# A four-layer graph network with a planned instruction order: layer 3 gathered by nodes, one flip through HBM, norms on ScalarE, scalings on GpSimd

## The chip, the cores and the metric

The kernel runs on one core of a Trainium2 chip. The core has TensorE (PE, with weight loads listed as PEld), VectorE (DVE), ScalarE (ACT), GpSimd (POOL) and the queues of SyncE (SP), which issue most of the DMAs here. The metric is device time in microseconds of one execution: 2461.91 us before, the median of three (2461.11 to 2462.0). Everything is fp32.

## The reference

There are 16 graphs (batches) of N = 1024 nodes with D = 128 features, and an adjacency with weights, about 1.6% of it nonzero. Four layers follow one another; each takes the layer-normed and ReLU'd state and adds its result to the state x, all per batch:

```
h = relu(layernorm(x))
layer 0, three times:  h = h @ W + b;  nh = h / |h|
                       h = (adj * (nh nh^T)) @ h;  relu but in the last;       x += h
layer 1:               x += mask * (relu(((1 + eps) h + adj^T h) @ W1 + b1) @ W2 + b2)
layer 2:               g = h @ W; attention over adj > 0 of tanh(g a1 + g a2), softmax;  x += attn @ g
layer 3:               g = h @ W^T + b;  e = g A g^T, plus its transpose
                       att = softmax(e where adj > 0 else 0, over the first node axis) * adj
                       hp = relu(att @ g)
                       i, f, o = sigmoid([h, hp] . w + b), three gates for each node
                       x += o * tanh(sigmoid(i * hp + f * h))
```

In layer 3 the three gates need, for each node, the dot product of hp with three rows of 128 weights (the second halves of the gate weights).

## The kernel before

**Tiles.** A batch's state is one tile of 128 partitions by 1024: eight blocks of 128 nodes, nodes on partitions, features along the row. Where a product needs features on partitions the tile is flipped: `flipped` (L619) transposes eight blocks on TensorE (L562) into PSUM and takes them out with two ScalarE evictions (L615). `squares` (L566) does the same by another way: it writes the tile to HBM, reads it back in 32 by 32 squares and turns the squares with one VectorE transpose. The adjacency lies in SBUF as eight row tiles adjT (128 x 1024, turned by the same trick on loading, `turn`, L859), and for layer 1 as loaded (adjL).

**The loops.** For each batch, `layer0` to `layer3` run over eight blocks j. In layers 0 and 3 `Square.row` (L741) makes a row of a symmetric product in two PSUM tiles of 128 x 512 (L753), taking blocks below the diagonal from already computed ones, by transposes on TensorE (L763) from copies `above`, or, in the middle batches, through HBM (`by_hbm`, `got`). VectorE multiplies that row with adjT into a tile ew or e (L952, L1169), and TensorE gathers it. There are two ways to gather. `accumulate` (L810) holds h of block j as weights and streams 512 columns of e twice: the result comes out with features on partitions. `accumulate_nodes` (L820) holds one 128 x 128 block of e at a time as weights and streams 128 columns of h, eight times: the result comes out with nodes on partitions. Layer 3 uses the first, so its result hpT must be turned back: `project` (L587) multiplies it with eye3, an identity with the three gate weight columns beside it (131 columns), which gives hp and the gates' dot products at once (psN, L1213), and ScalarE copies them out (L1216).

**Norms and gates.** `layernorm` (L653) takes statistics on VectorE (L663, L672), the power -1/2 on GpSimd (rstd, L555), and scales the first four blocks on VectorE (L691) and the other four on ScalarE with the ReLU inside (L698); `relu` (L712) does the ReLU of the first four. Layer 0's row norms rn are powers on GpSimd too. Layer 2 adds `alone` times hn to x, for nodes without neighbours (L1035, L637). Layer 3's `finish` (L1225) makes the gates (L1237, L1261, L1262), multiplies hn with f on GpSimd (L1265), then i * hp + z and o * z + x: on VectorE, eight `scalar_tensor_tensor` each (L1255), and in the last two batches on GpSimd (L1248, L1249). Then the result leaves by DMA. In the last batch this goes in two halves. In the last two batches GpSimd also multiplies the odd rows e with adjT (L1190).

**The order of the work.** Nothing is issued as written. Every operation goes into a `Plan` (L54) with an engine and an estimated time, the planner chooses a static order for each engine, and the program is emitted in that order. Ready operations are ranked by a deadline of the batch (PERIOD, LAST), less the length of what follows them, less a lead from the table LEADS. Buffers come from pools (POOLS) with a limit in all, and one for batches younger than the oldest unfinished (KINDS). An operation with `port` set shares a resource with GpSimd's in the plan: it places no two of them at one time. FLAGS are letters that switch variants; before they are "Cabcdkxhyz".

## Time and profile before

| | busy us | share of the span of 2462.7 us |
|---|---|---|
| TensorE matmuls | 2397.5 | 97% |
| VectorE | 2106.1 | 86% |
| ScalarE | 1291.5 | 52% |
| GpSimd | 254.5 | 10% |

A line of the groups reads: the line of the code, the engine, the operation, output <- inputs with their shapes, how many; then the busy time in all and the mean in ns; then the idle time ahead of it and who ended it. A line of the chain or the timeline begins with its start and its length in us. An fp32 matmul stands as two records with a weight load each, so counts of matmuls are twice those of the code; transposes stand as one. Lines of the profile are those of the kernel before.

### The profile page before, as it was taken

The numbers are of one execution on the slowest core, as the hardware profiler recorded it, in microseconds if no ns is written. First come the engines' busy times: TensorE is split into PE (matmuls) and PEld (weight loads), VectorE is DVE, ScalarE is ACT, GpSimd is POOL, SyncE is SP. The second block draws the span as 40 slices with busy tenths as digits, with TensorE's granted clock in tenths as the row PEclk, the third lists the DMA queues.
The fourth block names the chain that finished last, engine by engine and source line by source line (L and its number), as shares of the span: only waits on it lengthen the run. The fifth ranks groups of instructions, "written<-read, shape, count | busy, mean of one in ns | idle before, by whom it ended". The sixth has DMA issues, their size and how long they took to land.

```text
span 2462.7 us, 34845 instructions
## 1 busy us (share of the span) xinstructions
PE 2397.5 (97%) x11946; PEld 1592.9 (65%) x11946; DVE 2106.1 (86%) x5232; ACT 1291.5 (52%) x2404; POOL 254.5 (10%) x155
## 2 busy tenths in 40 slices
PE   6999999999999999999999999999999999999985
PEld 3568576775756657576675766657576675765763
DVE  6758889888998989899898998989899898897585
ACT  4415564735546465464644646465464745656274
POOL 1001010100101101010010101101010010100025
PEclk9999999999999999999999999999999999999998
DMA  8731929658394764928649394774929646072000
GB/s 132 125 103 35 167 56 144 139 89 160 72 159 112 107 142 94 174 67 147 136 82 167 65 164 114 100 145 93 173 73 146 134 86 133 28 96 75 26 1 18
DMA packets 1129473, 263.35 MB, mean 107 GB/s; under 512 B 971856, under 2 KB 1112912, under 8 KB 1129296
## 3 DMA queue, kind: packets, MB, share of 16 engines
q1 hardware_dynamic: 1108368, 251.73, 57.3%
q10 hardware_dynamic: 20928, 9.40, 1.4%
q8 instruction: 94, 1.54, 0.3%
q14 instruction: 83, 0.68, 0.1%
HBM read 198.14 MB, written 62.91 MB: 106 GB/s over the span
## 4 chain that ended last, share of the span: by engine, by line
PE 86%; DVE 5%; DMA 4%; ACT 3%; SPq 1%; POOL 1%; issue 0%; POOLq 0%; DVEq 0%; ACTq 0%
PE acc L815 33%; PE sq L753 17%; PE acc L826 17%; PE psP L593 6%; PE sq L763 4%; PE py L1014 2%; PE py L603 2%; PE ps_hTn L562 2%; DMA adjT<-in_adj_dram 1%; DMA by_hbm<-above 1%; PE ps_hnT L562 1%; PE pg L603 1%; DVE ew L952 1%; PE psN L593 1%; SPq L872 1%; DMA got<-by_hbm 1%
## 5 line engine op out<-in xcount | busy, mean ns | idle before, releaser
L952 DVE SCALAR_TENSOR_TENSOR ew<-sq,rn,adjT 128x512 f32<-128x512 f32 x612 | 437.9, 741 | 92.8 <-ACT above L785 33.0
L815 PE MATMUL acc<-ew,h 128*128 128x512 f32 x1024 | 488.0, 598 | 8.6 <-DVE ew L952 8.3
L753 PE MATMUL sq<-hTn 128*128 128x512 f32 (+3 forms) x1152 | 432.3, 488 | 0.4 <-ACT hTn L615 0.3
L785 ACT COPY above<-sq 128x384 f32<-128x384 f32 (+3 forms) x432 | 167.6, 392 | 431.8 <-PE sq L763 257.4
L753 PEld LDWEIGHTS sq<-hTn 128*128 128x128 f32 x1152 | 198.8, 191 | 152.6 <-issue 104.3
L815 PEld LDWEIGHTS acc<-ew,h 128*128 128x128 f32 x1024 | 177.7, 191 | 164.8 <-issue 120.9
L555 POOL TENSOR_TENSOR rstd<-ve,mhalf 128x8 f32<-128x8 f32 x64 | 107.5, 1679 | 1572.5 <-DVE ve L674 1524.3
L826 PEld LDWEIGHTS acc<-h,ew 128*128 128x128 f32 x2048 | 243.1, 192 | 29.9 <-issue 17.3
L826 PEld LDWEIGHTS acc<-h,e 128*128 128x128 f32 x2048 | 240.5, 194 | 25.6 <-issue 13.3
L826 PE MATMUL acc<-h,ew 128*128 128x128 f32 x2048 | 252.3, 276 | 0.9 <-DVE ew L952 0.9
L826 PE MATMUL acc<-h,e 128*128 128x129 f32 x2048 | 243.1, 277 | 3.4 <-DVE e L1102 3.4
L815 PE MATMUL acc<-e,hs 128*128 128x512 f32 x512 | 242.1, 595 | 0.5 <-DVE e L1194 0.5
L883 ACT ACTIVATE adjT<-adjT 128x1024 f32<-128x1024 f32 x128 | 135.2, 1057 | 203.8 <-DVE adjT L880 136.2
L815 PE MATMUL acc<-adjL,hn 128*128 128x512 f32 x512 | 229.6, 593 | 0.1
L763 PEld LDWEIGHTS sq<-ident,above 128*128 128x128 f32 x960 | 125.2, 141 | 122.1 <-issue 79.2
L1185 ACT ACTIVATE e<-e,top 128x1024 f32<-128x1024 f32 x128 | 146.8, 1147 | 105.3 <-DVE top L1181 103.6
L763 PE MATMUL sq<-ident,above 128*128 128x128 f32 x960 | 175.5, 274 | 5.5 <-ACT above L785 5.4
L1102 DVE SCALAR_TENSOR_TENSOR e<-adjT,e 128x512 f32<-128x512 f32 x256 | 161.5, 685 | 14.6 <-ACT e L1098 14.4
L880 DVE STREAM_TRANSPOSE adjT<-adjT 128x1024 f32<-128x1024 f32 x128 | 154.5, 1223 | 14.5 <-DMA adjT<-in_adj_dram 13.9
L775 DVE STREAM_TRANSPOSE above<-sq 128x512 f32<-128x512 f32 x208 | 147.3, 709 | 21.6 <-PE sq L753 19.6
L815 PEld LDWEIGHTS acc<-adjL,hn 128*128 128x128 f32 x512 | 93.9, 190 | 102.8 <-issue 88.1
L1194 DVE TENSOR_TENSOR e<-e,adjT 128x512 f32<-128x512 f32 x240 | 157.2, 686 | 0.0
(129 smaller groups left out, 3534.2 us busy)
## 6 DMA issues: line engine op xcount, KB each, us to landing
adjT<-in_adj_dram SPq DMA_DIRECT2D x512, 128.0 KB, 4.2
adjL<-in_adj_dram SPq DMA_DIRECT2D x128, 512.0 KB, 5.0
by_hbm<-above SPq DMA_DIRECT2D x104, 512.0 KB, 4.1
got<-by_hbm SPq DMA_DIRECT2D x416, 128.0 KB, 3.9
x<-in_x_dram SPq DMA_DIRECT2D x15, 512.0 KB, 5.4
out_dram<-z ACTq DMA_DIRECT2D x15, 512.0 KB, 5.9
x<-in_x_dram SPq DMA_DIRECT2D x2, 256.0 KB, 4.4
out_dram<-z ACTq DMA_DIRECT2D x2, 256.0 KB, 2.3
```

What stands on the lines that cost most here:

```text
L593: nc.tensor.matmul(dst.t[:, (c - lo) * n : (c - lo + 1) * n], cols(srcT.t, c), w, start=True, stop=True)
L753: lambda: nc.tensor.matmul(dst.t[:, (first - lo) * P :], cols(leftT.t, j), span(rightT.t, first, hi), start=True, stop=True),
L763: nc.tensor.transpose(cols(dst.t, r), cols(above.t, p), ident)
L775: lambda: nc.vector.transpose(span(above.t, p, p + 4), read.t),
L785: lambda: nc.scalar.copy(span(above.t, p, p + hi - first), read.t[:, (first - lo) * P :]),
L815: lambda s=s, lo=lo, hi=hi: nc.tensor.matmul(acc[s].t, cols(h.t, at, w), span(ew.t, lo, hi), start=(j == 0), stop=(j == NB - 1)),
L826: nc.tensor.matmul(a.t[:, (c - lo) * n : (c - lo + 1) * n], cols(ew.t, c), h.t[:, j * w : j * w + n], start=(j == 0 and c == lo), stop=(j ...
L880: dve(V(N), [t], [t], lambda t=t: nc.vector.transpose(t.t, t.t), True)
L952: lambda view=view, ew=ew, rn=rn, j=j, lo=lo, hi=hi: nc.vector.scalar_tensor_tensor(by_block(span(ew.t, lo, hi), D, 4), view(), rn.t[:, j ...
L1102: lambda e=e, j=j, lo=lo, hi=hi: nc.vector.scalar_tensor_tensor(span(e.t, lo, hi), span(aT[j].t, lo, hi), 0.0, span(e.t, lo, hi), op0=ALU. ...
L1185: lambda e=e, top=top, tot=tot: nc.scalar.activation(e.t[:, 0:N], e.t[:, 0:N], AF.Exp, bias=top.t, accum_out=tot.t),
L1194: lambda e=e, j=j, lo=lo, hi=hi: nc.vector.tensor_mul(span(e.t, lo, hi), span(e.t, lo, hi), span(aT[j].t, lo, hi)),
```

## The change

Five letters come in by FLAGS, and "y" goes, as P takes in what it did:

- **E**: in batches 0 to 13 layer 3 is gathered by nodes. hp comes out with nodes on partitions, so the eight products with eye3 and their copies go. The gates' dot products are made by three GpSimd multiplications of hp with a weight row (wh3, loaded once, repeated over the blocks), each with a VectorE sum along the features.
- **R**: norms are scaled on ScalarE alone, eight activations with the ReLU inside; the separate ReLU goes.
- **P**: layer 2's `alone` and layer 3's two scalings run on GpSimd, as a multiplication and an addition over the whole tile, but for the last batch's layer 3.
- **D**: from batch 2 on layer 0's first flip is made through HBM, by `squares`.
- **T**: in the last batch layer 3's scalings and the odd rows' multiplications run on VectorE; batch 14 keeps them on GpSimd.

It is for taking work from TensorE and VectorE and giving it to the engines with idle time. The plan's numbers change with it: the pools, limits, PERIOD, LAST, WINDOW, some estimates of GpSimd times, and the whole table of leads, which is left out here.

```diff
--- before.py
+++ after.py
@@ -288,6 +288,7 @@
 
         return loaded(group, name, [P, n], src.partition_broadcast(P))
 
+    FLAGS = set("CabcdkxhERPDzT")
     R = B * NB
     w0, b0 = [], []
     for i, (w, v) in enumerate(((L0_W0, L0_b0), (L0_W1, L0_b1), (L0_W2, L0_b2))):
@@ -312,12 +313,16 @@
     w3e = const.tile([D, E3], F32, name="w3e")
     b3e = const.tile([P, E3], F32, name="b3e")
     eye3 = const.tile([D, E3], F32, name="eye3")
+
+    wh3 = const.tile([P, 3 * D], F32, name="wh3") if "E" in FLAGS else None
     load_const(third, b3e[:, 0:D], L3_W_b.partition_broadcast(P))
     for g, (w, v) in enumerate(((L3_ig_w, L3_ig_b), (L3_fg_w, L3_fg_b), (L3_og_w, L3_og_b))):
         at = slice(D + g, D + g + 1)
         load_const(third, w3e[:, at], w[0, 0:D].rearrange("(p o) -> p o", o=1))
         load_const(third, eye3[:, at], w[0, D : 2 * D].rearrange("(p o) -> p o", o=1))
         load_const(third, b3e[:, at], v.partition_broadcast(P))
+        if "E" in FLAGS:
+            load_const(third, wh3[:, g * D : (g + 1) * D], w[0, D : 2 * D].partition_broadcast(P))
     for load_it in first:
         load_it()
     maskf = const.tile([R, P], F32, name="maskf")
@@ -330,136 +335,137 @@
     bg = const.tile([D, 1], F32, name="bg")
 
 
-    POOLS = {"adjT": 16, "adjL": 5, "x": 3, "big": 13, "above": 2, "got": 1, "bank": 8, "small": 29, "row": 8, "hbm": 3, "hrow": 2}
+    POOLS = {"adjT": 16, "adjL": 5, "x": 3, "big": 13, "above": 2, "got": 1, "bank": 8, "small": 22, "row": 6, "hbm": 3, "hrow": 2}
     KINDS = {
-        "adjT": ("adjT", 16, 16), "adjL": ("adjL", 5, 5), "x": ("x", 3, 3), "w4": ("big", 10, 6),
-        "chunk": ("big", 12, 4), "above": ("above", 2, 1), "got": ("got", 1, 1), "ps": ("bank", 8, 8),
-        "acc": ("bank", 8, 8), "small": ("small", 7, 6), "row": ("row", 4, 2), "hbm": ("hbm", 3, 2),
+        "adjT": ("adjT", 16, 16), "adjL": ("adjL", 5, 5), "x": ("x", 3, 3), "w4": ("big", 9, 5),
+        "chunk": ("big", 13, 9), "above": ("above", 2, 1), "got": ("got", 1, 1), "ps": ("bank", 7, 7),
+        "acc": ("bank", 6, 6), "small": ("small", 7, 7), "row": ("row", 5, 2), "hbm": ("hbm", 3, 2),
         "hrow": ("hrow", 2, 1),
     }
-    PERIOD, LAST, AHEAD, WINDOW = 60.0, 9.0, 2, 0.05
+    PERIOD, LAST, AHEAD, WINDOW = 108.0, 34.0, 2, 0.02
 
     LEADS = {
...
     }
     plan = Plan(POOLS, KINDS, lambda b: min(b * PERIOD, (B - 2) * PERIOD + LAST), AHEAD, WINDOW, LEADS)
     now = [0, ""]
@@ -514,7 +520,6 @@
 
 
 
-    FLAGS = set("Cabcdkxhyz")
 
     LO, HI = 1, 2
     TINY = 0.09
@@ -648,7 +653,7 @@
 
         v = lambda: by_block(a.t, w)[:, :, 0:D]
         pool_op(1.9, [a, scalar], [a], lambda: nc.gpsimd.tensor_mul(v(), v(), per_node(of_node())))
-        pool_op(1.9, [a, b], [dst], lambda: nc.gpsimd.tensor_add(by_block(dst.t), v(), by_block(b.t)))
+        pool_op(2.37, [a, b], [dst], lambda: nc.gpsimd.tensor_add(by_block(dst.t), v(), by_block(b.t)))
 
     def layernorm(k, xt, behind=None):
 
@@ -817,20 +822,20 @@
                 ),
             )
 
-    def accumulate_nodes(acc, parts, h, j, w, n, ew):
+    def accumulate_nodes(acc, parts, h, at, w, n, ew, j):
 
         for a, (lo, hi) in zip(acc, parts):
 
             def emit(a=a, lo=lo, hi=hi):
                 for c in range(lo, hi):
                     nc.tensor.matmul(
-                        a.t[:, (c - lo) * n : (c - lo + 1) * n], cols(ew.t, c), h.t[:, j * w : j * w + n],
+                        a.t[:, (c - lo) * n : (c - lo + 1) * n], cols(ew.t, c), h.t[:, at * w : at * w + n],
                         start=(j == 0 and c == lo), stop=(j == NB - 1), skip_group_check=True,
                     )
 
             pe(
                 (hi - lo) * (MM_BLOCK + (n - P) * 4 / 2400),
-                [blk(h, j, j + 1, w), blk(ew, lo, hi)], [a], emit,
+                [blk(h, at, at + 1, w), blk(ew, lo, hi)], [a], emit,
             )
 
 
@@ -962,7 +967,7 @@
                 if i < 2:
                     accumulate(acc, h, j, D, ew, j)
                 else:
-                    accumulate_nodes(acc, HALVES, h, j, D, D, ew)
+                    accumulate_nodes(acc, HALVES, h, j, D, D, ew, j)
             if i < 2:
                 hT = w4(f"hT_{b}_{i + 1}")
                 for s, (lo, hi) in enumerate(HALVES):
@@ -1104,7 +1109,7 @@
                     ),
                     True,
                 )
-            accumulate_nodes(acc, THIRDS, h, j, E2, D + 1, e)
+            accumulate_nodes(acc, THIRDS, h, j, E2, D + 1, e, j)
         rden = small(f"rden_{b}", NB)
         o = w4(f"o_{b}")
         for a, (lo, hi) in zip(acc, THIRDS):
@@ -1158,6 +1163,7 @@
             hT = flipped(h, f"h3T_{b}", w=E3)
         square = Square(k, gT, hT, "d" in FLAGS and LO <= b < B - HI)
         acc = [bank(f"acc3_{b}_{s}") for s in range(2)]
+        by_nodes = "E" in FLAGS and b < B - 2
         for j in range(NB):
             e = chunk(f"e3_{b}_{j}")
             for s, (lo, hi) in enumerate(HALVES):
@@ -1186,9 +1192,9 @@
                     e.t[:, 0:N], e.t[:, 0:N], AF.Exp, bias=top.t, accum_out=tot.t
                 ),
             )
-            if ("5" in FLAGS or "z" in FLAGS and b >= B - 2) and j % 2:
-                pool_op(1.96, [e, aT[j]], [e], lambda e=e, j=j: nc.gpsimd.tensor_mul(e.t[:, 0:N], e.t[:, 0:N], aT[j].t))
-            for lo, hi in () if ("5" in FLAGS or "z" in FLAGS and b >= B - 2) and j % 2 else HALVES:
+            if ("5" in FLAGS or "z" in FLAGS and (b == B - 2 if "T" in FLAGS else b >= B - 2)) and j % 2:
+                pool_op(2.45, [e, aT[j]], [e], lambda e=e, j=j: nc.gpsimd.tensor_mul(e.t[:, 0:N], e.t[:, 0:N], aT[j].t))
+            for lo, hi in () if ("5" in FLAGS or "z" in FLAGS and (b == B - 2 if "T" in FLAGS else b >= B - 2)) and j % 2 else HALVES:
                 dve(
                     V(HALF), [blk(e, lo, hi), blk(aT[j], lo, hi)], [blk(e, lo, hi)],
                     lambda e=e, j=j, lo=lo, hi=hi: nc.vector.tensor_mul(
@@ -1202,13 +1208,32 @@
                 0.3, [tot, blk(h, j, j + 1, E3)], [hs],
                 lambda hs=hs, tot=tot, j=j: nc.scalar.activation(hs.t, cols(h.t, j, E3), AF.Copy, scale=tot.t),
             )
-            accumulate(acc, hs, 0, D, e, j)
-        hpT = w4(f"hpT_{b}")
+            if by_nodes:
+                accumulate_nodes(acc, HALVES, hs, 0, D, D, e, j)
+            else:
+                accumulate(acc, hs, 0, D, e, j)
+        hpT = None if by_nodes else w4(f"hpT_{b}")
+
+        hp = w4(f"hp_{b}")
         for s, (lo, hi) in enumerate(HALVES):
-            evict(acc[s], hpT, lo, hi, AF.Relu)
-
-        hp = w4(f"hp_{b}")
-        for lo, hi in THIRDS:
+            evict(acc[s], hp if by_nodes else hpT, lo, hi, AF.Relu)
+        z = w4(f"z_{b}")
+        share = small(f"share_{b}", 3 * NB)
+        for g in range(3) if by_nodes else ():
+            scaled_h = z
+            pool_op(
+                1.9, [hp], [scaled_h],
+                lambda g=g, scaled_h=scaled_h: nc.gpsimd.tensor_mul(
+                    by_block(scaled_h.t), by_block(hp.t), per_feature(wh3[:, g * D : (g + 1) * D])
+                ),
+            )
+            dve(
+                V(N), [scaled_h], [share],
+                lambda g=g, scaled_h=scaled_h: nc.vector.reduce_sum(
+                    share.t.rearrange("p (c g) -> p c g", g=3)[:, :, g], by_block(scaled_h.t), axis=AX.X
+                ),
+            )
+        for lo, hi in () if by_nodes else THIRDS:
             pn = ps(f"psN_{k}_{lo}")
             project(hpT, lo, hi, eye3, pn)
             act(
@@ -1219,8 +1244,8 @@
             )
 
         gate = small(f"gate_{b}", 3 * NB)
-        z = w4(f"z_{b}")
-        late = b >= B - 2
+        late = b == B - 2 if "T" in FLAGS else b >= B - 2
+        final = "T" in FLAGS and b == B - 1
 
         def finish(lo, hi):
             n = hi - lo
@@ -1233,6 +1258,12 @@
                 return by_block(t.t[:, lo * w :], w, n)[:, :, 0:D]
 
             def both():
+                if by_nodes:
+                    nc.vector.tensor_add(
+                        gate.t.rearrange("p (c g) -> p c g", g=3), share.t.rearrange("p (c g) -> p c g", g=3),
+                        by_block(h.t, E3)[:, :, D:],
+                    )
+                    return
                 v = gate.t[:, 3 * lo : 3 * hi].rearrange("p (c g) -> p c g", g=3)
                 nc.vector.tensor_add(v, by_block(hp.t[:, lo * E3 :], E3, n)[:, :, D:], by_block(h.t[:, lo * E3 :], E3, n)[:, :, D:])
 
@@ -1243,10 +1274,10 @@
 
             def scaled(a, w, g, c):
 
-                if "P" in FLAGS or ("y" in FLAGS and late):
+                if not final and ("P" in FLAGS or ("y" in FLAGS and late)):
                     us = 0.2 + 1.7 * n / NB
                     pool_op(us, [blk(a, lo, hi, w), at], [blk(a, lo, hi, w)], lambda: nc.gpsimd.tensor_mul(part(a, w), part(a, w), per_node(of(g), n)))
-                    pool_op(us, [blk(a, lo, hi, w), blk(c, lo, hi)], [blk(z, lo, hi)], lambda: nc.gpsimd.tensor_add(part(z), part(a, w), part(c)))
+                    pool_op(us + 0.4 * n / NB, [blk(a, lo, hi, w), blk(c, lo, hi)], [blk(z, lo, hi)], lambda: nc.gpsimd.tensor_add(part(z), part(a, w), part(c)))
                     return
 
                 def emit():
@@ -1257,14 +1288,22 @@
                 dve(n * STT, [blk(a, lo, hi, w), at, blk(c, lo, hi)], [blk(z, lo, hi)], emit, True)
 
             v = lambda: gate.t[:, 3 * lo : 3 * hi]
-            dve(TINY, [blk(hp, lo, hi, E3), blk(h, lo, hi, E3)], [at], both, True)
+            dve(TINY, [share if by_nodes else blk(hp, lo, hi, E3), blk(h, lo, hi, E3)], [at], both, True)
             act(0.22, [at], [at], lambda: nc.scalar.activation(v(), v(), AF.Tanh, scale=0.5))
             dve(TINY, [at], [at], lambda: nc.vector.tensor_scalar(v(), v(), 0.5, 0.5, op0=ALU.mult, op1=ALU.add), True)
-            pool_op(
-                0.2 + 1.7 * n / NB, [blk(hn, lo, hi), at], [blk(z, lo, hi)],
-                lambda: nc.gpsimd.tensor_mul(part(z), part(hn), per_node(of(1), n)),
-            )
-            scaled(hp, E3, 0, z)
+            if final:
+
+                def of_x():
+                    for k in range(lo, hi):
+                        nc.vector.tensor_scalar_mul(cols(z.t, k), cols(hn.t, k), gate.t[:, 3 * k + 1 : 3 * k + 2])
+
+                dve(n * 0.17, [blk(hn, lo, hi), at], [blk(z, lo, hi)], of_x)
+            else:
+                pool_op(
+                    0.2 + 1.7 * n / NB, [blk(hn, lo, hi), at], [blk(z, lo, hi)],
+                    lambda: nc.gpsimd.tensor_mul(part(z), part(hn), per_node(of(1), n)),
+                )
+            scaled(hp, D if by_nodes else E3, 0, z)
             act(S(n * P) + S(n * P, True), [blk(z, lo, hi)], [blk(z, lo, hi)], squash)
             scaled(z, D, 2, xt)
             op(
```

## The prediction

> **What bounds the kernel now.** I read the page first, for the engines' totals and the chain that ended last.
>
> ```profile
> PE 2397.5 (97%) x11946; PEld 1592.9 (65%) x11946; DVE 2106.1 (86%) x5232; ACT 1291.5 (52%) x2404; POOL 254.5 (10%) x155
> ...
> PE 86%; DVE 5%; DMA 4%; ACT 3%; SPq 1%; POOL 1%; issue 0%; POOLq 0%; DVEq 0%; ACTq 0%
> ```
>
> TensorE is the suspect, with VectorE (86% busy) the second. Busy shares are averages, so next came the windows: start, middle, end. Columns are the stretch, its length, then busy time of PE, PEld, DVE, ACT, POOL, the granted clock, the DMA share and GB/s.
>
> ```profile
> 0.00:80.00 80.00, 58.51 (x243) 34.90 (x244) 53.90 (x140) 37.34 (x73) 8.92 (x11) 0.96 0.99 138
> 80.00:2350.00 2270.00, 2261.08 (x11323) 1504.91 (x11322) 1976.84 (x4942) 1187.82 (x2212) 202.81 (x120) 1.00 0.60 111
> 2350.00:2463.00 113.00, 77.89 (x383) 53.07 (x381) 75.38 (x153) 66.36 (x121) 42.78 (x24) 0.85 0.03 10
> ```
>
> In 2270 us of middle TensorE is idle 8.9 us; the start has 21.5 us of idle and the end 35.1. PE's own waits in 861 to 1898 us sum to 2.7 us. A modelled end can hide a gap, so I checked that the matmuls run at their own rate, in the chain in order of time (start, length, what):
>
> ```profile
> 334.99 14.29 PE acc L826 x128
> ...
> 719.42 10.30 PE acc L815 x24
> ...
> 1904.68 10.30 PE acc L815 x24
> ...
> 2399.40 0.87 PE ps_h3T L562 x8
> ...
> 2434.80 1.80 PE psN L593 x16
> ```
>
> Each fp32 matmul is two records, a transpose one. So a 128x512 matmul takes 2 x 10.30/24 = 0.858 us, a 128x128 one 2 x 14.29/128 = 0.223, a transpose 0.87/8 = 0.109, and the eight psN matmuls 1.80 us. The same piece stands at 719.42 and, eight batches on, at 1904.68: 148.16 us per batch. The middle is paced by TensorE's issue and nothing else, so a microsecond of TensorE work removed there is a microsecond of span, if no other engine takes over.
>
> **What the skill says.** "Perfetto Trace Analysis", section "Identifying the Most-Contended Engine", warns that matmul busy time is no measure of headroom; the issue rates above carry my argument instead. "Matmuls" on that page says larger matmuls are more efficient: here four 128-column ones take 0.893 us against 0.858 for one of 512, so it agrees, at 4%. "SBUF — State Buffer", section "SBUF: two separate sides", says VectorE and GpSimd share a port pair as an exclusive lock: a VectorE operation with two SBUF inputs, or in a two-port mode, and a GpSimd one block each other for the whole instruction. The trace agrees: four L691 operations, 1.11 us undisturbed (timeline, 1005.03), took 3.15 us beside a GpSimd one:
>
> ```profile
> 2386.25 3.15 DVE L691 TENSOR_SCALAR hn<-x,mv,rstd 128x128 f32<-128x128 f32 x4
> ...
> 2386.41 2.38 POOL L1190 TENSOR_TENSOR e<-e,adjT 128x1024 f32<-128x1024 f32 x1 [0.70 <-PE sq L763]
> ```
>
> **The change part by part.** "E" acts in batches 0 to 13, "D" in 2 to 15, "R" and "P" in all (P's scaling of z not in batch 15, and batch 14 had it already).
>
> *E, layer 3 by nodes.* TensorE loses the eight psN matmuls, 1.80 us, and runs 16 products of 128x512 as 64 of 128x128: 16 x (0.893 - 0.858) = +0.56. Net -1.24 us a batch. ScalarE loses three copies (1.35 us: 21.6/16). GpSimd gains three multiplications of 128x1024, VectorE three reductions. The groups give prices:
>
> ```profile
> L1181 DVE TENSOR_REDUCE top<-e 128x1 f32<-128x1024 f32 x128 | 153.8, 1212 | 0.6
> ...
> L637 DVE SCALAR_TENSOR_TENSOR x<-hn,alone,x 128x128 f32<-128x128 f32 x128 | 34.9, 346 | 3.7 <-ACT hn L719 3.6
> ...
> L1265 POOL TENSOR_TENSOR z<-hn,gate 128x1024 f32<-128x1024 f32 x15 | 28.6, 1908 | 177.5 <-PE pf L1057 94.9 <-DVE gate L1262 51.8 <-PE sq L753 20.8
> L1190 POOL TENSOR_TENSOR e<-e,adjT 128x1024 f32<-128x1024 f32 x8 | 20.1, 2515 | 56.9 <-ACT e L1185 56.2 <-PE sq L763 0.7
> ```
>
> A broadcast multiplication on GpSimd is not shown with this pattern: between 1.91 us (one factor repeated) and 2.5 (two whole tiles, lock included). I take 1.91, since wh3 is also repeated: 5.7 us. Reductions: 3 x 1.15 (1.21 less the overlap of neighbours) = +3.4 us. The new chain multiply, reduce, multiply runs through one buffer z, some 10 us before the gates; the output alone waits for it, and holding hp, h and z that long is hidden while the limit of nine "w4" tiles is not reached.
>
> *D, layer 0's first flip through HBM.* TensorE -8 x 0.109 = -0.88 us; ScalarE loses two evictions, 1.19; VectorE gains one transpose of 128x1024, +1.15 to 1.22. Half a MB is written and half a MB read in 128-byte pieces; the DMA share of 0.60 in the middle leaves room. The write waits on SyncE's queue for hn, and behind it stand adjT loads and got reads, for which VectorE waits. Its latency, about 4 + 4 us of transfer (the by_hbm and got rows) and 1.2 of transpose, replaces some 2 us. Layer 0 of a batch needs only x, so it can start a layer early; I put it at zero.
>
> *R, norms on ScalarE.* VectorE loses 16 tensor_scalars at 0.28 us: -4.4. ScalarE gains 16 x 0.41 = 6.6 (four in 1.65 us) less three ReLUs of 0.62: +4.7. ScalarE is busy 79 of 148 us; E and D give back 2.5. Hidden, except that a norm comes out up to 1.6 us later in the first and last batch.
>
> *P.* VectorE loses 8 operations in layer 2 and 16 in layer 3, at 0.27 us (eight in 2.18): -6.5. GpSimd gains 3 x 1.91 + 2.2 + 2 x 2.34 = 12.6, about 12.5.
>
> Sums per middle batch: TensorE -2.12. VectorE 3.4 + 1.2 - 4.4 - 6.5 = -6.3, so 133.9 (the window 861 to 1009) falls to 127.6 of a 146 us period. GpSimd +18.2, to about 31.5. The lock decides: GpSimd's 31.5 us must lie beside VectorE work that doesn't need the pair. Some 83 us of VectorE's time reads PSUM or one operand (by the groups' rows, a batch: ew and e from sq 33, transposes of sq 8, reductions 16, statistics 9, additions from PSUM 17), and the rest, about 45, plus 31.5 is well under 146. Before, too, the order puts rstd (1.64 us) beside PSUM work. What can grow is a wait of rn in GpSimd's queue behind a 2 us multiplication; layer 0's ew wait for rn, and TensorE for them. I add 0.1 us a batch.
>
> *T and the end.* Now the last GpSimd chain ends the program:
>
> ```profile
> 2442.89 2.05 POOL L1265 TENSOR_TENSOR z<-hn,gate 128x512 f32<-128x512 f32 x2
> ...
> 2454.09 1.90 POOL L1248 TENSOR_TENSOR z<-z,gate 128x1024 f32<-128x1024 f32 x1
> 2456.07 2.34 POOL L1249 TENSOR_TENSOR z<-z,x 128x1024 f32<-128x1024 f32 x1
> ```
>
> From 2442.89 to 2454.09 GpSimd does batch 15's ten half-size operations, 11.2 us, before it finishes batch 14. T gives these to VectorE: 24 operations of 0.27, 6.6 us. Without them batch 14 waits only for its two tanhs (2.2 us), a gain of 11.2 - 2.2 = 9. But the VectorE operations need the pair too; if they alternate wholly with GpSimd's last five (10.3 us), 17 us replace 21.5: 4.5. Batch 15 also multiplies four odd blocks on VectorE again (+4.8 us, where VectorE is 23.6 of 25 us busy), and R and P take 6 off it earlier. Net gain 6, bounds 1 and 10.
>
> *Start.* Three more parameter rows of 64 KB each, and a first norm later by about 0.7 us, under a start that waits for adjT loads: 0, bounds -6 and +6. The new pools, limits and leads change the order; the profile doesn't price that.
>
> Sum: 14 x 2.12 = 29.7 off, 6 off, 1.4 added: 2461.9 - 34.3 = **2427.6**, so 2427.
>
> **Rivals.**
> - *Part is eaten (2441).* GpSimd's lock and its late rn give TensorE 1 us more idle per batch: +14. For it: GpSimd's load more than doubles. Against: VectorE gets lighter, and there was only 0.35 us of idle per batch at 90% VectorE.
> - *Better (2408).* VectorE's relief also shortens the start (21.5 us idle) and the wait of 9 us in 2350 to 2400, about 20 us together. For: in that stretch VectorE is 42.6 of 50 us busy. Against: the start waits for loads, which the change doesn't lighten.
> - *Nothing gained (2462).* Idle of 2.5 us a batch takes it all.
> - *Slower (2473).* If every added GpSimd microsecond blocked VectorE, it would be 127.6 + 18.2 = 145.8 of 146: no slack, and each late piece reaches TensorE. At 3.3 us of new idle a batch, 14 x 3.3 = 46: 2473. Against: most VectorE work doesn't need the pair.
>
> **How the numbers follow.** The forecast has 0.65, part eaten 0.13, better 0.09, nothing 0.03, slower 0.10. From 2404 to 2450 holds the first three with their bounds (start 6, end 5, 0.5 us a batch), leaving out "nothing", "slower" and a little of "better": about 0.16. Faster 0.87, same 0.03, slower 0.10.
>
> **What would show it.** Right: no psN before the last two batches; a period of 146.0 us between like pieces; TensorE's idle still near 9 us in the middle; VectorE near 127 us a batch; the last GpSimd operation ending 12 to 18 us after the last matmul, now 22. Wrong: TensorE waits for ew or e rows in the middle, rn rows with a long idle behind GpSimd multiplications, VectorE rows grown above 0.7 us, or SyncE waiting for hn ahead of adjT.

## The result and the profile after

The kernel after takes 2491.45 us (2489.07 to 2492.52), the kernel before 2461.51 (median of four executions): a ratio of 1.012 [1.0103, 1.0138]. It is 30 us slower; 34 us faster was forecast. The experiments below have another few executions of the kernel before beside them, with medians from 2462.4 to 2463.8, and their ratios are to these. The page of the kernel after, its engines and its chain:

```profile
PE 2398.7 (96%) x12954; PEld 1676.1 (67%) x12954; DVE 2102.3 (84%) x4712; ACT 1320.0 (53%) x2542; POOL 537.8 (22%) x271
...
PE 56%; DVE 19%; ACT 11%; DMA 7%; SPq 3%; issue 1%; POOL 1%; ACTq 0%; DVEq 0%
```

TensorE's share of the chain fell from 86% to 56%, VectorE's and ScalarE's rose from 5% to 19% and from 3% to 11%. VectorE was to become lighter by some 6 us a batch and shows the same total (2106.1 before, 2102.3 now). The windows, with the columns of those before (stretch, length, PE, PEld, DVE, ACT, POOL, clock, DMA share, GB/s):

```profile
0.00:80.00 80.00, 57.03 (x196) 31.77 (x197) 47.91 (x120) 35.70 (x76) 8.90 (x11) 0.94 0.84 132
80.00:2350.00 2270.00, 2223.05 (x12179) 1568.05 (x12178) 1953.12 (x4324) 1195.42 (x2299) 497.92 (x245) 1.00 0.61 117
2350.00:2490.00 140.00, 118.67 (x582) 76.24 (x580) 101.31 (x270) 88.90 (x168) 30.99 (x15) 0.96 0.06 19
```

In the middle TensorE is idle for 47 us of 2270, where it was 8.9. The chain in order of time gives the period: the same piece of layer 0 stands at 1174.00 and, five batches on, at 1928.74.

```profile
1174.00 2.84 PE acc L820 x6
...
1928.74 2.84 PE acc L820 x6
```

That is 754.74 / 5 = 150.9 us a batch: 148.2 before, 146.0 forecast. Busy rows can hide gaps, so I added up, over all neighbouring matmuls of each trace, the time from start to start less the rate of that form. What is left is TensorE's idle time. The 12 us ahead of the first matmul are left out, since they are the same in both:

| us | before | after | difference | forecast |
|---|---|---|---|---|
| TensorE's work at its own rate | 2358.9 | 2328.8 | -30.1 | -29.7 |
| its idle time between first and last matmul | 66.0 | 138.3 | +72.3 | +1.4 |
| after its last matmul | 25.6 | 10.5 | -15.1 | -6 |
| span of the profiled run | 2462.7 | 2489.5 | +26.8 | -34.3 |

The work is gone as forecast. The loss is 72 us of new waiting, 5 us a batch. The longest waits of PE from 861 to 1898 us, seven batches (2.7 us in all before):

```profile
PE acc L820 <- DVE ew L957: 16.8, 21, 1.8
PE ps_hnT L567 <- ACT hn L703: 3.9, 5, 1.2
PE psP L598 <- ACT hnT L620: 1.7, 7, 0.2
```

Layer 0's gathering waits for ew from VectorE. Why is ew late? First the groups of VectorE, before, then after, and GpSimd's new group (busy us, mean ns of one):

```profile
L952 DVE SCALAR_TENSOR_TENSOR ew<-got,rn,adjT 128x512 f32<-128x512 f32 x156 | 112.1, 746 | 10.4 <-DMA got<-by_hbm 6.0 <-DMA adjL<-in_adj_dram 3.3 <-issue 0.5
L997 DVE TENSOR_TENSOR adjL<-adjL,ident_e 128x128 f32<-128x128 f32 x128 | 35.3, 293 | 11.9 <-DMA adjL<-in_adj_dram 10.4 <-PE acc L815 1.5
L1050 DVE TENSOR_SCALAR hrow<-hsum 128x128 f32<-128x128 f32 x16 | 4.5, 282 | 0.0
```

```profile
L957 DVE SCALAR_TENSOR_TENSOR ew<-got,rn,adjT 128x512 f32<-128x512 f32 x156 | 132.5, 885 | 34.6 <-DMA got<-by_hbm 32.9
L1002 DVE TENSOR_TENSOR adjL<-adjL,ident_e 128x128 f32<-128x128 f32 x128 | 63.8, 522 | 7.0 <-DMA adjL<-in_adj_dram 7.0
L1055 DVE TENSOR_SCALAR hrow<-hsum 128x128 f32<-128x128 f32 x16 | 21.0, 1313 | 13.1 <-ACT hnT L620 13.1
```

```profile
L1226 POOL TENSOR_TENSOR z<-hp,wh 128x1024 f32<-128x1024 f32 x42 | 103.7, 2469 | 542.9 <-ACT hp L620 495.0 <-DVE share L1232 46.6 <-DVE mv L677 1.3
```

The same VectorE instructions, with the same shapes, are longer: ew from `got` 885 ns against 746, the adjL additions 522 against 293, hrow 1313 against 282. Summed over all VectorE instructions that are more than 50 ns longer than the median of their form before, the time above that median is 85.0 us in the kernel after and 5.0 in the kernel before. That is why VectorE did not become lighter. The timeline shows one case (start, length, idle ahead and its releaser in brackets):

```profile
1064.31 4.16 DVE L957 SCALAR_TENSOR_TENSOR ew<-got,rn,adjT 128x512 f32<-128x512 f32 x3
1064.46 2.79 POOL L1226 TENSOR_TENSOR z<-hp,wh 128x1024 f32<-128x1024 f32 x1 [2.00 <-DVE share L1232]
1067.85 1.12 PE L820 MATMUL acc<-ew,h 128*128 128x512 f32 x2 [0.88 <-DVE ew L957]
```

Three ew operations with two SBUF operands take 4.16 us beside one GpSimd multiplication of 2.79, where the mean before gives 3 x 0.746 = 2.2. One by one in the trace they take 0.74, 2.83 and 0.74 us: the second lasts until 1067.80, past the end of the multiplication at 1067.25. TensorE's next piece waits 0.88 us for this second one.

The same rows show one thing more. VectorE's ew also wait for `got`, the transfers back from HBM: 32.9 us, and 6.0 before. That is no stretching, and it comes back below. The end did get shorter: GpSimd closes at 2453.92, and VectorE ends the program, where GpSimd did before.

```profile
2451.54 2.37 POOL L1280 TENSOR_TENSOR z<-z,x 128x1024 f32<-128x1024 f32 x1
2485.00 1.14 DVE L1286 SCALAR_TENSOR_TENSOR z<-z,gate,x 128x128 f32<-128x128 f32 x4 [0.40 <-ACT z L1273]
```

### The profile page after: what moved, and what is told of

Its sections match the earlier page's. It is cut to its first block, busy times and chain, and to the rows that moved or that the text cites. A ratio compares the mean times of both kernels' runs of the same rounds, so it can differ in the third digit from the quotient of the medians.

```text
span 2489.5 us, 36784 instructions
## 1 busy us (share of the span) xinstructions
PE 2398.7 (96%) x12954; PEld 1676.1 (67%) x12954; DVE 2102.3 (84%) x4712; ACT 1320.0 (53%) x2542; POOL 537.8 (22%) x271
## 4 chain that ended last, share of the span: by engine, by line
PE 56%; DVE 19%; ACT 11%; DMA 7%; SPq 3%; issue 1%; POOL 1%; ACTq 0%; DVEq 0%
PE acc L831 16%; PE acc L820 15%; PE sq L758 12%; DVE ew L957 6%; PE psP L598 4%; SPq L811 3%; ACT hn L703 3%; PE sq L768 3%; DMA got<-by_hbm 2%; ACT e L1099 2%; PE py L608 2%; DMA by_hbm<-above 2%; DVE x L642 2%; DVE e L1175 2%; DVE share L1232 1%
## 5 line engine op out<-in xcount | busy, mean ns | idle before, releaser
L820 PE MATMUL acc<-ew,h 128*128 128x512 f32 x1024 | 482.0, 600 | 33.3 <-DVE ew L957 33.0
L703 ACT ACTIVATE hn<-x,nb,rstd 128x128 f32<-128x128 f32 x512 | 205.8, 482 | 81.6 <-DVE nb L687 81.4
L831 PEld LDWEIGHTS acc<-h,e 128*128 128x128 f32 x2048 | 234.4, 192 | 17.5 <-issue 9.9
L831 PE MATMUL acc<-h,e 128*128 128x129 f32 x2048 | 235.8, 275 | 2.0 <-DVE e L1107 2.0
L831 PEld LDWEIGHTS acc<-hs,e 128*128 128x128 f32 x1792 | 212.4, 193 | 21.4 <-issue 20.5
L1226 POOL TENSOR_TENSOR z<-hp,wh 128x1024 f32<-128x1024 f32 x42 | 103.7, 2469 | 542.9 <-ACT hp L620 495.0
L831 PE MATMUL acc<-hs,e 128*128 128x128 f32 x1792 | 217.7, 276 | 2.1 <-DVE e L1200 2.1
L560 POOL TENSOR_TENSOR rn<-ss,mhalf 128x8 f32<-128x8 f32 x48 | 89.0, 1855 | 588.5 <-DVE ss L944 579.5
```

Source lines behind the costliest of these rows:

```text
L560: pool_op(1.64, [src], [dst], lambda: nc.gpsimd.tensor_tensor(dst.t, src.t, mhalf, op=ALU.pow))
L703: nc.scalar.activation(cols(hn.t, c), cols(xt.t, c), AF.Relu, bias=nb.t[:, c : c + 1], scale=rstd.t[:, c : c + 1])
L820: lambda s=s, lo=lo, hi=hi: nc.tensor.matmul(acc[s].t, cols(h.t, at, w), span(ew.t, lo, hi), start=(j == 0), stop=(j == NB - 1)),
L831: nc.tensor.matmul(a.t[:, (c - lo) * n : (c - lo + 1) * n], cols(ew.t, c), h.t[:, at * w : at * w + n], start=(j == 0 and c == lo), stop=( ...
L1226: lambda g=g, scaled_h=scaled_h: nc.gpsimd.tensor_mul(by_block(scaled_h.t), by_block(hp.t), per_feature(wh3[:, g * D : (g + 1) * D])),
```

## The experiments

My theory after the result: the idle time comes from GpSimd's new instructions, which stretch VectorE instructions by the lock, and from the norms, which now take longer. Rivals: D's transfers delay the flips; the slower part is E's longer chain; the changed order costs by itself; GpSimd's own instructions (rn, rstd) come late behind its new work. A changed estimate or letter lets the planner make quite another order, and then two things differ at once. So in all experiments but three (e4, e11, e12) the planned order of every engine is that of the kernel which the run edits, instruction by instruction, and only the body of an instruction differs.

### GpSimd's new work made small: e1, e2, e3

```diff
 # e1: the gates' three multiplications on 8 columns; the sums read hp
-  nc.gpsimd.tensor_mul(by_block(scaled_h.t), by_block(hp.t), per_feature(wh3[:, g * D : (g + 1) * D]))
+  nc.gpsimd.tensor_mul(scaled_h.t[:, 0:8], hp.t[:, 0:8], wh3[:, g * D : g * D + 8])
 # e2: P's multiplications and additions on 8 columns, for instance
-  nc.gpsimd.tensor_mul(v(), v(), per_node(of_node()))
+  nc.gpsimd.tensor_mul(a.t[:, 0:8], a.t[:, 0:8], of_node())
 # e3: both
```

> The changed kernel with the order of every engine kept, but the three GpSimd multiplications per batch for layer 3's gates shrunk from 128x1024 to 128x8, and the sums taken over hp instead of z (so the gates are not the reference's). Theory 'lock' (GpSimd's time blocks VectorE through the shared port pair, TensorE then waits for ew): these were 7.4 us of 18.2 added a batch; some 1.5 to 2.5 us of the 5.0 us of new TensorE idle go, so 2491 falls to about 2457 to 2470. Theory 'order' (the new static order makes TensorE wait whatever GpSimd does): within 6 us of 2491.

> The changed kernel with every order kept, but the six GpSimd scalings of a batch (layer 2's multiplication and addition for nodes without neighbours, layer 3's two multiplications and two additions) shrunk from 128x1024 to 128x8; their results are left out of the rest of the tile. Theory 'lock': 12.7 of the added 18.2 us a batch go, so 2.5 to 3.5 us of idle a batch: 2440 to 2457. Theory 'order': within 6 us of 2491 but for the tail, where batch 14's scalings end the program: about 2483.

> The changed kernel with every order kept and both kinds of GpSimd work shrunk to 128x8, the gates' multiplications and the scalings (their results are left out). Theory 'lock': the middle period falls from 150.8 to 146 to 146.8 us and the time to 2425 to 2437, as the prediction had it without the lock. Theory 'order': the period stays over 149 us and the time over 2475. In between the two share the cause, and the period says in what proportion.

| | us | ratio to before | TensorE idle | VectorE time lost to stretched instructions |
|---|---|---|---|---|
| after | 2491.45 | 1.012 [1.0103, 1.0138] | 138.3 | 85.0 |
| e1 | 2462.01 | 0.9996 [0.9987, 1.0004] | 110.8 | 47.4 |
| e2 | 2480.82 | 1.0073 [1.0058, 1.0088] | 126.0 | 43.6 |
| e3 | 2454.75 | 0.9969 [0.9959, 0.998] | 100.8 | 8.3 |

E's three multiplications cost 29 us of span, P's six operations 11, both 37. e1 lies where the lock theory had it; e2 and e3 gain less than that theory said, e2 about what its rival forecast, and in e3 the period is 147.7 us (layer 1's first product stands at 1015.21 and, six batches on, at 1901.63), 3.2 of the 4.9 us by which 150.9 exceeds the forecast. The rest of the period is not GpSimd's new work. Each takes about half of the stretching with it, but not the same half. In e2 the groups of VectorE read:

```profile
L957 DVE SCALAR_TENSOR_TENSOR ew<-got,rn,adjT 128x512 f32<-128x512 f32 x156 | 131.6, 879 | 32.9 <-DMA got<-by_hbm 28.5 <-PE sq L758 2.5 <-issue 0.2
L1002 DVE TENSOR_TENSOR adjL<-adjL,ident_e 128x128 f32<-128x128 f32 x128 | 43.8, 366 | 5.0 <-DMA adjL<-in_adj_dram 5.0
L1055 DVE TENSOR_SCALAR hrow<-hsum 128x128 f32<-128x128 f32 x16 | 5.0, 311 | 28.7 <-ACT hnT L620 28.7
```

hrow is at 311 ns again and the adjL additions at 366, but ew stays at 879. In e1 it is the other way: ew 752, hrow 1223, adjL 503. So P stretches hrow and the adjL additions, for which TensorE does not wait in the list above, and E stretches ew, for which it does. So 38 us of stretching are worth 29 us of span in one place and 41 are worth 11 in the other. P's 11 may have another road: VectorE's wait for rn, which a busy GpSimd gives late, is 16.3 us in the kernel after and 10.3 in e2 (9.0 before), and e2 doesn't separate it from the stretching. E's chain of multiplications and sums is shorter in e1 too, but ew does not come from it, and VectorE waits for these products for only 2.1 us in the whole kernel after.

TensorE's wait for ew doesn't vanish in e1: over the same stretch of time it falls from 16.8 us in 21 waits to 9.0 in 7, one a batch. That one is at the piece by which I read the period, at 1174.00 in the kernel after, and nothing is stretched there. It is still there when everything is short (e6, below).

### The same operation with another repetition: e10

Was it the size of E's multiplications, 2.47 us each where I had taken 1.91, or that they were there at all?

```diff
-  nc.gpsimd.tensor_mul(by_block(scaled_h.t), by_block(hp.t), per_feature(wh3[:, g * D : (g + 1) * D]))
+  nc.gpsimd.tensor_mul(by_block(scaled_h.t), by_block(hp.t), per_node(wh3[:, g * D : g * D + NB]))
```

> The kernel after with its order kept; its three multiplications for the gates' dot products repeat one factor per node along the features (the form priced at 1.91 us) in place of a row of weights repeated over the nodes; the gates are then not the reference's. Same bytes, engines and waits. Theory (the lock costs, not the size of the operation): the mean goes from 2.47 us to 2.0 or 2.2, blocked VectorE still reads two SBUF operands beside it, and of the 29 us that the shrunk multiplications gave back only 4 to 10 come back: 2481 to 2488. Rival (the operation was mis-sized, and 1.91 us each would have fitted into the gaps): 20 us or more come back, 2463 to 2471.

It takes 2473.99 us, ratio 1.0041 [1.0027, 1.0055], 17 us less than the kernel after, with 121.8 us of idle. The group of GpSimd:

```profile
L1226 POOL TENSOR_TENSOR z<-hp,wh 128x1024 f32<-128x1024 f32 x42 | 84.2, 2005 | 546.8 <-ACT hp L620 494.5 <-DVE share L1232 50.5 <-DVE mv L677 1.8
```

The mean goes from 2469 to 2005 ns by nothing but the operand's repetition: one factor along 128 features in place of a row of 128 along eight blocks. In both runs the third of a batch's three is itself held up beside VectorE; around 1050 to 1062 us the two others take 2.36 and 2.35 us in the kernel after, and 1.90 each in e10. That removes 19.5 us of GpSimd time and 17 us of span; VectorE's stretching falls from 85.0 to 72.8. My theory expected 4 to 10 us; the rival, 20 or more, was nearer. So of E's 29 us some 17 are the mis-sized operation and 12 the rest of it.

### The lock alone, in two places: e8 and e9

The kernel before, with its order kept; three GpSimd multiplications of a tile that nobody reads are added in batches 2 to 15. e8 puts them behind layer 0's first row norm, e9 behind layer 1's rstd. In a middle batch GpSimd has nothing else to do for 39 and 40 us then.

```diff
+    spare = const.tile([P, N], F32, name="spare")
+    nc.vector.memset(spare, 1.0)
 ...
             power(rn, ss)
+            if i == 0 and b >= 2:                       # e8
+                plan.ops[-1].also = 3
 ...
         power(rstd, ve)
+        if k.endswith("_1") and k not in ("0_1", "1_1"):    # e9, in place of that
+            plan.ops[-1].also = 3
 ...
             o.fn()
+            for _ in range(getattr(o, "also", 0)):
+                nc.gpsimd.tensor_mul(by_block(spare), by_block(spare), per_feature(ident))
```

> The kernel before, its order kept, with three GpSimd multiplications of 128x1024 on a tile that nothing else uses, a batch, in batches 2 to 15, put behind layer 0's first rn, where GpSimd is idle for 39 us: only the port pair is disturbed. Theory 'the lock alone costs TensorE time': 14 x 1 to 2 us: 2475 to 2490. Rival 'VectorE's slack takes the blocked time up, and the changed kernel loses because its order has none': under 2467.

> The kernel before with its order kept, and three GpSimd multiplications of 128x1024 more in batches 2 to 15, on a tile that nobody reads, as in the run before it; but now they stand behind layer 1's power (rstd), where VectorE adds adjL and ident_e and multiplies ew or e rows from SBUF, and where GpSimd then is free for about 40 us. Theory (the lock is what costs, and it costs by what VectorE does beside it): VectorE operations with two SBUF operands stretch, its time lost to blocked instructions grows from 5 to 25 us or more (it was 8.6 with the same work beside PSUM reads), TensorE's idle in the middle from 2.0 to 3 or 4 us a batch, and the time is 2475 to 2495. Rival (GpSimd's load costs the same wherever it stands): as the run before, 2472, with blocked time near 9 us. Rival (a few us of VectorE are hidden by the order's slack): 2462 to 2466.

e8 takes 2472.06 us, 1.0037 [1.0025, 1.0048]. e9 takes 2569.65, 1.0439 [1.0423, 1.0454]: the same instructions in another place cost 107 us instead of 9. The timeline of e8, then that of e9:

```profile
1266.71 7.25 POOL L1365 TENSOR_TENSOR spare<-spare,ident 128x1024 f32<-128x1024 f32 x3
1267.19 0.71 DVE L956 SCALAR_TENSOR_TENSOR ew<-sq,rn,adjT 128x512 f32<-128x512 f32 x1
1267.83 0.70 DVE L777 STREAM_TRANSPOSE above<-sq 128x512 f32<-128x512 f32 x1
1268.45 1.37 DVE L956 SCALAR_TENSOR_TENSOR ew<-sq,rn,adjT 128x512 f32<-128x512 f32 x2
```

```profile
1035.08 7.25 POOL L1365 TENSOR_TENSOR spare<-spare,ident 128x1024 f32<-128x1024 f32 x3
1035.20 2.25 DVE L686 SCALAR_TENSOR_TENSOR nb<-mv,rstd 128x8 f32<-128x8 f32 x1
1037.37 5.29 DVE L695 TENSOR_SCALAR hn<-x,mv,rstd 128x128 f32<-128x128 f32 x4
1042.69 0.63 ACT L723 ACTIVATE hn<-hn 128x512 f32<-128x512 f32 x1 [3.56 <-DVE hn L695]
1043.38 2.08 PE L819 MATMUL acc<-adjL,hn 128*128 128x512 f32 x2 [5.28 <-ACT hn L723]
```

In e8 VectorE works on PSUM beside the multiplications. An ew from sq takes 0.71 us (mean before 0.741), the transposes 0.70 and 0.71: nothing is stretched (8.6 us in the whole run), and TensorE's idle in seven middle batches is 14.6 us, 13.9 without the load. The profiled run of e8 is 10.7 us longer than that of the kernel before, and compared with it matmul by matmul, it loses 9.4 of them in two places. Once, at 506 us, the three multiplications stand ahead of a rstd in GpSimd's queue, which begins at 513.25 where it was 507.14; layer 3's norm is late, and TensorE waits for it:

```profile
506.08 7.21 POOL L1365 TENSOR_TENSOR spare<-spare,ident 128x1024 f32<-128x1024 f32 x3
513.25 1.64 POOL L557 TENSOR_TENSOR rstd<-ve,mhalf 128x8 f32<-128x8 f32 x1
515.49 2.01 PE L564 MATMUL ps_hnT<-ident,hn 128*128 128x128 f32 x8 [3.96 <-DVE hn L693]
```

That costs 5.9 us and is no lock, but GpSimd's own queue. The other 3.5 us come near the end, from 2179 us on, where the multiplications meet VectorE's e with two SBUF operands (2.53, 1.12 and 1.04 us, mean before 0.68 and 0.69) and TensorE waits 2.29 us for one of them. So where the load meets PSUM reads alone, in the middle, it costs under 1 us in seven batches.

In e9 nb and hn come next. They took 0.13 and 1.11 us in the kernel before (timeline, 1004.99 and 1005.03) and take 2.25 and 5.29 here, 6.3 us more. One by one the four hn take 0.33, 2.36, 2.50 and 0.33 us: the second and the third each last until one of GpSimd's multiplications is over. The chain is then in the open: ReLU after hn, and layer 1's first product after the ReLU, 5.28 us late. The waits of PE in 861 to 1898:

```profile
PE acc L819 <- ACT hn L723: 37.0, 7, 5.3
```

That is 5.3 us in each of seven batches; counted from start to start, as in the table above, TensorE's idle time ahead of these products is 101 us in the whole run, 7.2 for each of 14 batches. The 42 added instructions sum to 99.3 us on GpSimd, stretched ones gain 87 us on VectorE, and the profiled span grows by 104.9. The theory was right in kind and far too low (2475 to 2495): at a VectorE instruction for which TensorE waits at once, a microsecond of GpSimd is about a microsecond of span.

### The norms made short, and D: e5, e6, e7

```diff
 # e5: half a norm as one activation of 128x512, with one factor for the half
-  for c in range(lo, hi):
-      nc.scalar.activation(cols(hn.t, c), cols(xt.t, c), AF.Relu, bias=nb.t[:, c : c + 1], scale=rstd.t[:, c : c + 1])
+  nc.scalar.activation(span(hn.t, lo, hi), span(xt.t, lo, hi), AF.Relu, bias=nb.t[:, lo : lo + 1], scale=rstd.t[:, lo : lo + 1])
 # e6: e3 and e5
 # e7: e6, and D's way back from HBM as one plain transfer, so that hT is no flip any more
-  for g in range(P // SQ): nc.sync.dma_start(...)      # four reads of squares
+  nc.sync.dma_start(by_block(dst.t), d.t.rearrange("(c p) f -> p c f", p=P))
```

> The changed kernel, every order kept, with each half of a norm scaled in one ScalarE activation of 128x512 in place of four of 128x128 (one block's mean and scale for four blocks, so the norms of the others are wrong): a norm takes about 1.3 us of ScalarE in place of 3.3. TensorE's idle in front of the flips that wait for hn is 10.7 us of 48.7 in seven middle batches. Theory 'the norm's latency is a share of the cause': 1.5 us a batch goes, 16 x 1.5 = 24 us less than the changed kernel's 2491: 2464 to 2472. Rival 'those waits only stand in front of the one for ew, which comes anyway': within 6 us of 2491.

> The changed kernel, every order kept, with the gates' multiplications, the scalings and the norms all short (their results left out or wrong). Both kinds of GpSimd work short gave 2454.8. If the norm's latency adds up with them: 2430 to 2440, a middle period near 147. If what is left is the order or the transfers: 2449 or more.

> As the kernel with three things short, and layer 0's flip through HBM read back in one plain transfer in place of four of 128-byte pieces (the features are then not in their places): SyncE has three issues of some 0.85 us a batch less, and 512 KB comes in larger pieces. If SyncE's queue and the small pieces make got and adjT late, and VectorE with them: 8 to 20 us under the kernel with three short. If the transfers lie hidden: within 4 us of it.

e5: 2472.41 us, 1.0039 [1.0024, 1.0054]; e6: 2437.2, 0.99 [0.9884, 0.9917]; e7: 2436.76, 0.9896 [0.9881, 0.9911]. The timelines of the kernel after and of e5 show what was shortened:

```profile
1073.26 3.19 ACT L703 ACTIVATE hn<-x,nb,rstd 128x128 f32<-128x128 f32 x8 [0.60 <-DVE nb L687]
```

```profile
1062.02 1.52 ACT L702 ACTIVATE hn<-x,nb,rstd 128x512 f32<-128x512 f32 x2 [0.60 <-DVE nb L687]
```

A norm of eight blocks takes 3.19 us on ScalarE, and 1.52 with two large activations. That gives 19 us back. Before, VectorE and ScalarE did half each at one time; layer 2's norm:

```profile
1196.87 1.11 DVE L691 TENSOR_SCALAR hn<-x,mv,rstd 128x128 f32<-128x128 f32 x4
1197.04 1.65 ACT L698 ACTIVATE hn<-x,nb,rstd 128x128 f32<-128x128 f32 x4 [0.95 <-DVE nb L682]
```

From the end of nb to the last block that layers 1, 2 and 3 wait for, the medians are 2.2 (with the ReLU), 1.7 and 2.7 us before, and 3.2, 3.2 and 3.7 after. So R makes three norms of a batch 1.0 to 1.5 us later. Layer 0's is no later than before: there the old order left 8.7 us for it, the new one takes 3.2. In e5 the medians are 1.6, 1.6 and 2.0, a little less than before, so 19 us is rather more than R's own price.

What TensorE loses shows in layer 3's flip, first before, then after:

```profile
1399.92 0.62 PE L562 MATMUL ps_hnT<-ident,hn 128*128 128x128 f32 x4
1421.18 1.48 PE L567 MATMUL ps_hnT<-ident,hn 128*128 128x128 f32 x4 [0.32 <-ACT hn L703]
```

Its first four transposes start 0.38 us apart, one for each activation of ScalarE, where it is 0.11 otherwise; before, VectorE had these four blocks ready. In seven middle batches, counted from start to start, the idle time ahead of psP falls from 8.9 to 1.2 us in e5 and that ahead of ps_hnT from 10.7 to 5.3. (The listed wait of ps_hnT for hn is 3.9 us in the kernel after and 4.3 in e5; it is the spacing that goes.) e5 also halves ScalarE's work for the norms, behind which its evictions stand, and doesn't separate this from the norm's length.

The three parts add up: 29 + 11 + 19 = 59, and e6 is 54 us below the kernel after. Of D's transfers the reads back are hidden: e7 has three issues fewer a batch on SyncE's queue, and the time is the same. It leaves the write of hn in that queue, which waits for hn for 142 us in e6 and in e7 alike.

In e6 one wait for ew is left in each batch, 8.1 us in seven batches, and no stretched instruction stands ahead of it:

```profile
1146.39 1.29 DVE L1174 SCALAR_TENSOR_TENSOR e<-adjT,got 128x512 f32<-128x512 f32 x2 [0.95 <-DMA adjT<-in_adj_dram]
1149.53 1.40 DVE L956 SCALAR_TENSOR_TENSOR ew<-sq,rn,adjT 128x512 f32<-128x512 f32 x2
1150.33 1.55 PE L819 MATMUL acc<-ew,h 128*128 128x512 f32 x3 [1.56 <-DVE ew L956]
```

Between the first two lines VectorE makes another e and a reduction of layer 3, and nb; layer 0's ew stands behind them, and the first of them waits 0.95 us for a transfer. The period of e6 is 147.3 us (from 1004.19 to 1887.84, six batches). No run changes this place, so what part the order has in it, and what part the transfers, stays open.

### T alone, and other orders: e4, e11, e12

e4 is the kernel before with T; only the order of the last two batches differs.

```diff
-    FLAGS = set("Cabcdkxhyz")
+    FLAGS = set("CabcdkxhyzT")      # with the change's lines for T
```

> The kernel before with the last part of the change alone: in the last batch layer 3's scalings and odd rows on VectorE, batch 14's on GpSimd. Its order differs from before only in the last two batches. If the 11.6 us that the changed kernel gains after the last batch's layer 1 come from this part: 2450 to 2454. The prediction's 6 us: 2456. If the gain came from the other parts or the new order of the end: 2460 or more.

2460.4 us, 0.9989 [0.998, 0.9998]. GpSimd's last instruction ends at 2424.7 where it was 2458.4, but the last matmul ends at 2451.0 and not at 2437.0. The waits of PE from 2380 us on:

```profile
PE acc L819 <- DVE e L1199: 14.7, 6, 6.7
```

T gives VectorE the odd rows' multiplications (e) again, and TensorE waits 14.7 us for them. In the kernel after the same wait is 5.1 us; there R and P have taken work from VectorE, and the order is another, and this run does not tell which of the two it is.

e11 and e12 compute all that the reference asks for. Each has a new table of leads, made for it with corrected costs, and new pools and limits; e11 has E, R, D and T, e12 only D and T.

```diff
 # e11 and e12
-    FLAGS = set("CabcdkxhERPDzT")
+    FLAGS = set("CabcdkxhyzEDRT")      # e12: "CabcdkxhyzDT"
-                1.9, [hp], [scaled_h],
+                2.45, [hp], [scaled_h],
-            dve(TINY, [ss], [ss], lambda ss=ss: ...)
+            dve(TINY, [ss], [ss], lambda ss=ss: ..., True)      # also alone, hrow
```

> The change without P (letters E, R, D, T; the scalings stay on VectorE and, in the last two batches, where the kernel before has them), nothing left out, and a new table of leads, sought with corrected costs: the gates' multiplications at 2.45 us instead of 1.9, a norm's half at 1.68 instead of 1.55, and three more VectorE operations marked as sharing a resource with GpSimd (hrow, alone, ss). By these costs the plan itself ends at 2429.7 (the plan of the kernel before at 2455.5, where the chip takes 2461.9; that of the kernel after at 2440.0, where the chip takes 2491). Theory (the idle time comes from an order made with wrong costs, not from the change): 2432 to 2445, idle of TensorE below 85 us, and VectorE's time lost to blocked instructions below 30 us. Rival (the change costs these waits in any order, since VectorE and GpSimd lie too close): 2455 or more, with blocked time as after, 60 to 90 us.

> The kernel before with D and T alone, nothing left out, and a table of leads sought for it: no new GpSimd work at all, TensorE with 14 x 0.88 = 12.3 us less, the last batch's scalings on VectorE. The plan ends at 2435.3. Theory (D's saving is real and its transfers cost nothing; without GpSimd's new work nothing blocks): 2438 to 2446, TensorE's work 12 us below before, idle 55 to 66 us, blocked time near 5 us. Rival (D's HBM route makes late flips, so that waits of psP and sq eat it): 2455 or more.

e11: 2459.67 us (2454.82 to 2463.12), 0.9988 [0.9981, 0.9995]; e12: 2447.4 us, 0.9937 [0.992, 0.9953], the fastest kernel here with the reference's whole work. The groups of GpSimd and the waits of PE in e11:

```profile
L1661 POOL TENSOR_TENSOR z<-hp,wh 128x1024 f32<-128x1024 f32 x42 | 104.1, 2478 | 514.2 <-ACT hp L1055 454.9 <-DVE share L1667 59.2
```

```profile
PE acc L1255 <- DVE ew L1392: 20.1, 10, 8.2
PE ps_hT L1002 <- ACT hn L1138: 11.2, 1, 11.2
```

The multiplications are as long as in the kernel after (2478 ns). Stretching is 40.2 us and idle 103.1, after had 85.0 and 138.3. But P is missing here, so e2, with P's GpSimd work small, is the fair neighbour: 43.6 and 126.0. The new order and the marks did not lessen the stretching; it fell on instructions for which TensorE waits less, 23 us of idle. The theory missed its 2432 to 2445, and the rival's time, 2455 or more, held, though not its 60 to 90 us of stretching: TensorE still waits 20.1 us for ew, where it was 8.3 before and 33.0 in the kernel after. (The single wait of 11.2 us is the program's first norm, 11.9 before.) Whether some order gives E its full saving stays open. e12 has no new GpSimd work: TensorE's work is 2347.0 us (11.9 less than before; 14 x 0.88 = 12.3), stretching 13.5, idle 76.8, and 10.8 us remain after the last matmul. D's saving and T's shorter end arrive, 12 and 15 us; 11 of them go to new idle time, and 15 us of span are gained. I had expected 2438 to 2446, with 55 to 66 us of idle. No run gives the kernel before a new table of leads alone, so what the table itself brings is not shown.

## Why the prediction was wrong

**The work of TensorE: right.** 30.1 us gone, 29.7 forecast; psN is left in batches 14 and 15 only.

**E's multiplications, "I take 1.91, since wh3 is also repeated": wrong.** 2.47 us, near the upper end of my bounds, and 2.36 where nothing held them. wh3 is repeated the other way, over blocks and not along the features, and no row of the kernel before showed that. e10 prices the error at 17 us. The range named both ends, but the sum for the span used a capacity in which 0.56 us more could not matter.

**The lock, "the rest, about 45, plus 31.5 is well under 146": the step that failed.** That is a sum of loads, and loads could be placed side by side only if both engines were free to choose. VectorE takes its instructions in a fixed order: when the one at its head needs the pair while GpSimd works, it and all behind it wait, and what stands behind it may be the ew that TensorE wants next. The Trainium skill, "SBUF — State Buffer", section "SBUF: two separate sides", says that each of the two blocks the other for its whole instruction; I cited that, and then priced it as if it met only the average. The runs agree with the page on which instructions meet: two SBUF operands or a tensor_scalar stretch (e9), those with a PSUM source and one SBUF operand do not (e8). Measured: 80 us more of stretched VectorE time, and 37 us of span from E and P together (e3), where I had put 1.4. For E's 29 of them it is not GpSimd's own queue: VectorE waits 16.3 us for rn and 28 for rstd in the kernel after and in e1 alike. My rival "slower" had the right sign, with 46 us of new idle time where it was 72. But its cause, that every added GpSimd microsecond blocks VectorE, is not what happened: GpSimd gained 283 us (537.8 less 254.5), and VectorE's stretching is 80.

**R, "Hidden, except that a norm comes out up to 1.6 us later in the first and last batch": wrong.** The three norms of layers 1 to 3 are 1.0 to 1.5 us later, within my 1.6, but every batch pays for it: the flips ps_hnT go at the pace of ScalarE's activations, and what follows waits for them. e5: 19 us, a little more than R's own share. I had looked at ScalarE's load, 79 of 148 us, when the question was who waits for hn.

**P, free beside other work: wrong by 11 us** (e2). Whether by the lock or by rn, which comes later out of GpSimd's queue, is not shown. The prediction named the second, at 0.1 us a batch.

**D, at zero: right as far as it was tested.** The shorter reads back change nothing (e7), and TensorE's work falls as forecast (e12). That the write waits for hn in SyncE's queue was left in place in every run.

**T and the end, -6 within 1 to 10: the mechanism was right, the size too small.** After the last matmul 15.1 us are gone. But that time does not come by itself: in e4 T gains some 3 us, since TensorE then waits for the odd rows, while in e12's order it arrives without R and P. My 4.8 us for the odd rows were a load on VectorE; it is again the order that says what they cost.

**The start, at zero: not shown to be longer by itself.** The first matmul with layer 1's second weights in batch 2 (py, L1014 before, L1019 after) begins at 451.45 instead of 445.13 us. But it begins at 445.92 in e6, which loads the same parameters in the same order, so nearly all of these 6 us are the same waits of E, R and P.

Together: the kernel after is 63.9 us above the forecast of 2427.6. With E's and P's work on GpSimd and R's length taken out, e6 is 54.3 us faster, and 9.6 are left: TensorE idles 84.0 us there, where the forecast has 67.4, and 10.5 us after the last matmul, where it has 19.6. Of these 16.6 us of idle time some 11 are the wait for ew that e6 still shows, one a batch from 561 to 1887 us. So the cause is shown for most of the loss: E and P's work on GpSimd, and norms that come late. That last wait, which comes with the new order or with its transfers, stays open.

## What to carry to other kernels

When work moves to an engine that excludes another, don't compare the sums of their loads: list what stands at the head of the other engine's queue in that stretch, whether it needs what is shared, and who waits for it. The same seven microseconds of GpSimd work a batch cost 9 us in one place and 107 in another. Work that two engines did at once takes longer on one of them alone, even where that engine is half idle, so ask for its latency and for who waits for its first piece, and price an operation by a row with the same repetition of operands.

## What the runs showed of the hardware

- A GpSimd multiplication of 128x1024 takes 2.47 us with a row repeated over blocks and 2.00 with one factor repeated along the features (e10), in the same place of the same order; 2.36 and 1.90 us where neither engine held the other.
- The smallest instruction is held as long as a large one: nb, 128x8, took 2.25 us in e9 and 0.13 before. It ended at 1037.45, when the first of GpSimd's three instructions (7.25 us together from 1035.08) was over, at 1037.42.
- VectorE instructions with a PSUM source and one SBUF operand beside that (ew from sq) ran beside GpSimd at 0.71 us, no longer than its mean before, 0.741.
